# A graph network's second layer: edge features loaded into the ring, and gathers that add node rows to them

## The chip, the cores and the metric

The kernel runs on one core of a Trainium2 chip. The metric is the device time of one execution in microseconds; the kernel before takes 4083.93 us (median of 10 runs, 4080.28 to 4091.4). A core has TensorE (PE in the profile, with its weight loads PEld), VectorE (DVE), ScalarE (ACT), GpSimd (POOL) and SyncE (SP), each with its own instruction queue, and 16 DMA engines that all queues share. Here SP issues the plain loads and stores, and GpSimd issues the indirect gathers.

## What is computed

There are 12500 nodes with 128 features each and 200000 edges, sorted by destination. Two graph layers run one after the other, each followed by a residual addition and a normalization. The first is an attention layer. The second, cut to what matters:

```python
def _L1_gnn_ref(node_feat, edge_feat, src, dst, W1, b1, W2, b2):
    m = node_feat[src] + edge_feat
    neigh = jax.ops.segment_sum(m, dst, num_segments=node_feat.shape[0])
    h = 2.0 * node_feat + neigh
    h = h @ W1 + b1
    h = jnp.where(h > 0, h, 0.01 * h)
    return h @ W2 + b2
...
x = _layernorm(x + _L0_gnn_ref(x, edge_index, ...), axis=-1)
x = _layernorm(x + _L1_gnn_ref(x, edge_attr_128, src, dst, ...), axis=-1)
```

For every edge the second layer adds the source node's row and the edge's own feature row, both of 128 float32 numbers, and sums the result over the edges of each destination node.

## The kernel before, in words

The edges are cut into 112 chunks of 1792 edges (`CE` = 128 partitions x `T` = 14 tiles; the last chunk has 9 tiles). A tile is 128 edges, one per partition. Because edges are sorted by destination, a chunk touches a run of fewer than 128 destination nodes, so that the sum of a tile over its edges is one TensorE product: a 128x128 matrix of zeros and ones (edge by node, `od`), times the 128x128 rows of the tile, accumulated in PSUM (`ps`) over the tiles of the chunk. A node whose edges run over the end of a chunk is carried to the next chunk in a small product (`pc`).

A gather of one tile is one indirect DMA on GpSimd's queue (line 66, in `gather`): it reads 128 rows of 512 bytes from a table in HBM at the addresses in `srcs`, and writes them to one tile of a chunk's place in SBUF. A chunk is 14 such instructions, 64 KB each. The places are a ring of six (`ring`, `RING` = 6); chunk `c` uses place `c % 6`. Both layers gather through the same function and the same ring. The first layer gathers from `x_pad` and `xl_d`; its result `x1` is stored to `x1_d` in HBM by SP (line 567, in `norm2`), and stays in SBUF as `x1w`. The second layer gathers from `x1_d`, so that its first gather has to wait for the last of those stores.

The second layer is written out by hand in program order (the last loop of `fast_path`). Step `c` issues the load of the edge features of chunk `c + 2` (`load1`, lines 801 to 816, on SP, 896 KB), the 14 gathers of chunk `c + 1` (GpSimd), the making of `od` for chunk `c + 1` (`edges1`, on ScalarE, lines 240 and 241), and then the products of chunk `c` (`sums1`, line 823 on). Edge features go into a tile `ea` of their own, of which there are three. In `sums1` each tile takes two products with the same `od`, one with the edge features (line 827) and one with the gathered rows (line 828):

```python
nc.tensor.matmul(ps, od[:, t, :], ea[:, t, :], start=(t == 0), stop=False)
nc.tensor.matmul(ps, od[:, t, :], got[:, t, :], start=False, stop=(t == tiles[c] - 1))
```

Then VectorE adds twice the node's own row (line 833) and the carried row, and every fourth chunk `finish1` runs the two weight products, the normalization, and the stores of the output on SP (line 869). Those stores take their start row from a register that SP loads. The last chunk's output goes out by one indirect store on GpSimd (line 873).

Waits follow from the data. Each engine takes its queue in order, and an instruction whose operands are not ready holds up all behind it on its engine. A gather waits for the readers of its place in the ring (the products of the chunk six earlier) and, since eight completion counters are used in turn for GpSimd's DMAs, for the gather eight before it.

Of the kernel before, what the change touches and what calls it, by code (L numbers as in the profile page):

```python
# [8 lines left out]
F32 = mybir.dt.float32  # L9
# [3 lines left out]
OP = mybir.AluOpType  # L13
# [3 lines left out]
P = 128  # L17
D = 128
# [6 lines left out]
T = 14  # L25
# [4 lines left out]
RING = 6  # L30
# [6 lines left out]
def gnn_kernel(ctx: ExitStack, tc: tile.TileContext, a: dict, out: bass.AP):  # L37
# [3 lines left out]
    nc = tc.nc  # L41
    N = out.shape[0]
    E = a["edge_attr_128"].shape[0]
    NCH = a["dst_rows"].shape[0]
# [4 lines left out]
    tiles = [T] * (NCH - 1) + [-(-(E - (NCH - 1) * CE) // P)]  # L49
# [6 lines left out]
    srcs = const.tile([P, NCH, T], I32, name="srcs")  # L56
# [2 lines left out]
    nc.scalar.dma_start(srcs[:, 1:EARLY], src_of[:, 1:EARLY])  # L59
    ring = [const.tile([P, T, D], F32, name=f"got{i}") for i in range(EARLY)]  # L60

    def gather(table, c):

        got = ring[c % RING]
        for t in range(tiles[c]):
            nc.gpsimd.indirect_dma_start(  # L66
                out=got[:, t, :], out_offset=None, in_=table[:N, :],
                in_offset=bass.IndirectOffsetOnAxis(ap=srcs[:, c, t:t + 1], axis=0))
        return got

    for c in range(EARLY):
        gather(a["x_pad"], c)
# [30 lines left out]
    x1_d = dram.tile([NB * P + P, D], F32, name="x1_d")  # L103
# [109 lines left out]
    with tc.If(fits > 0) as cond:  # L213
        fast_path(tc, a, out, locals())
# [5 lines left out]
def fast_path(ctx: ExitStack, tc: tile.TileContext, a: dict, out: bass.AP, g: dict):  # L220
    nc = tc.nc
    N, E, NCH, groups, group_of = (g[k] for k in ("N", "E", "NCH", "groups", "group_of"))
    n0i, srcs, rel, same, lastf, thru, nid, khot, ident, wlr, xl_d, x1_d = (g[k] for k in (
        "n0i", "srcs", "rel", "same", "lastf", "thru", "nid", "khot", "ident", "wlr", "xl_d", "x1_d"))
    nnid, nrel, iota, rows, w12, b1, att, heads, tiles, ring, gather = (g[k] for k in (
        "nnid", "nrel", "iota", "rows", "w12", "b1", "att", "heads", "tiles", "ring", "gather"))
# [6 lines left out]
    def first_node(c, most=N):  # L233
        return nc.values_load(n0i[0:1, c:c + 1], engines=[ET.SP], min_val=0, max_val=most)

    def edge_by_node(od, c, t0, m):


        for t in range(t0, t0 + m):
            nc.scalar.activation(od[:, t, :], iota[:, 0, :], AF.Abs, bias=nrel[:, c, t:t + 1])  # L240
        nc.scalar.activation(od[:, t0:t0 + m, :], od[:, t0:t0 + m, :], AF.Relu, bias=1.0, scale=-1.0)  # L241

    def layernorm(w, of, n):
        st = w.tile([P, G, 6], F32, name="st")
        mv = w.tile([P, G, 2], F32, name="mv")
        for j in range(n):
            nc.vector.bn_stats(st[:, j, :], of[:, j, :])
            nc.vector.bn_aggr(mv[:, j, :], st[:, j, :])
        sd = w.tile([P, G], F32, name="sd")
        nc.scalar.activation(sd[:, :n], mv[:, :n, 1], AF.Sqrt, bias=eps)  # L250
        nc.vector.reciprocal(sd[:, :n], sd[:, :n])
        for j in range(n):
            nc.vector.tensor_scalar(of[:, j, :], of[:, j, :], mv[:, j, 0:1], sd[:, j:j + 1],
                                    op0=OP.subtract, op1=OP.mult)


    with tc.tile_pool(name="ew", bufs=2) as ew, \
# [425 lines left out]
        c, k, pool = NCH - 2, len(pairs) - 1, nc.gpsimd  # L683
# [112 lines left out]

    with tc.tile_pool(name="gw", bufs=2) as gw, \
            tc.tile_pool(name="gp", bufs=1, space=bass.MemoryType.PSUM) as gp:
        eas, gots, hs, ods = {}, {}, {}, {}

        def load1(c):
            ea = gw.tile([P, T, D], F32, name="ea", bufs=3)
            left = E - c * CE
            if left >= CE:
                nc.sync.dma_start(ea, a["edge_attr_128"][c * CE:(c + 1) * CE, :].rearrange(
                    "(p t) d -> p t d", t=T))
            else:
                m = tiles[c]
                full, more = left // m, left % m
                nc.vector.memset(ea[full // 32 * 32:, :m], 0.0)  # L810
                nc.sync.dma_start(ea[:full, :m], a["edge_attr_128"][c * CE:c * CE + full * m, :].rearrange(
                    "(p t) d -> p t d", t=m))
                if more:
                    nc.sync.dma_start(ea[full:full + 1, :more, :], a["edge_attr_128"][
                        None, c * CE + full * m:E, :])
            eas[c] = ea

        def edges1(c):
            ods[c] = gw.tile([P, T, P], F32, name="od")
            for t in range(0, tiles[c], 7):  # L820
                edge_by_node(ods[c], c, t, min(7, tiles[c] - t))

        def sums1(c):
            ea, got, od = eas.pop(c), gots.pop(c), ods.pop(c)
            ps = gp.tile([P, D], F32, name="ps", bufs=2)
            for t in range(tiles[c]):
                nc.tensor.matmul(ps, od[:, t, :], ea[:, t, :], start=(t == 0), stop=False)  # L827
                nc.tensor.matmul(ps, od[:, t, :], got[:, t, :], start=False, stop=(t == tiles[c] - 1))  # L828
            grp, j = group_of[c]
            if j == 0:  # L830
                hs[grp] = gw.tile([P, G, D], F32, name="h")
            h = hs[grp]
            nc.vector.scalar_tensor_tensor(h[:, j, :], x1w[:, c, :], 2.0, ps, op0=OP.mult, op1=OP.add)  # L833
            if c > 0:
                nc.vector.tensor_add(h[0:1, j, :], h[0:1, j, :], eas[-1])
            if c + 1 < NCH:
                ns = gw.tile([P, D], F32, name="ns")
                nc.scalar.copy(ns, ps)  # L838
                pc = gp.tile([1, D], F32, name="pc", bufs=2)
                nc.tensor.matmul(pc, khot[:, c:c + 1], ns, start=True, stop=True)  # L840
                eas[-1] = pc
            if j == grp[1] - 1:
                finish1(grp)

        def finish1(grp):
            c0, n = grp
            h, x1 = hs.pop(grp), x1w[:, c0:c0 + n, :]
            pT = gp.tile([P, G, P], F32, name="pT")
            for j in range(n):
                nc.tensor.transpose(pT[:, j, :], h[:, j, :], ident)  # L850
            hT = gw.tile([P, G, P], F32, name="hT")
            nc.scalar.copy(hT[:, :n], pT[:, :n])
            pu = gp.tile([P, G, P], F32, name="pu")
            nc.tensor.matmul(pu[:, :n], w12[:, 0, :], hT[:, :n], start=True, stop=True)
            z = gw.tile([P, G, P], F32, name="z")
            nc.scalar.activation(z[:, :n], pu[:, :n], AF.Identity, bias=b1)
            nc.vector.scalar_tensor_tensor(z[:, :n], z[:, :n], 0.01, z[:, :n],
                                           op0=OP.mult, op1=OP.max)
            po = gp.tile([P, G, D], F32, name="po")
            for j in range(n):  # L860
                nc.tensor.matmul(po[:, j, :], z[:, j, :], w12[:, 1, :], start=True, stop=True)
            nc.vector.tensor_add(x1, x1, rows["L1_gnn_b2"].to_broadcast([P, n, D]))
            y = gw.tile([P, G, D], F32, name="y")
            nc.vector.tensor_add(y[:, :n], po[:, :n], x1)
            layernorm(gw, y, n)
            for j in range(n):
                c = c0 + j
                if c + 1 < NCH:
                    nc.sync.dma_start(out[ds(first_node(c, N - P), P), :], y[:, j, :])
                else:  # L870
                    rows_i = gw.tile([P, 1], I32, name="rows_i", bufs=1)
                    nc.vector.tensor_copy(rows_i, nid[:, c:c + 1])
                    nc.gpsimd.indirect_dma_start(  # L873
                        out=out[:, :], out_offset=bass.IndirectOffsetOnAxis(ap=rows_i[:, 0:1], axis=0),
                        in_=y[:, j, :], in_offset=None, bounds_check=N - 1, oob_is_err=False)

        load1(0)
        load1(1)
        gots[0] = gather(x1_d, 0)
        edges1(0)  # L880
        for c in range(NCH):
            if c + 2 < NCH:
                load1(c + 2)
            if c + 1 < NCH:
                gots[c + 1] = gather(x1_d, c + 1)
                edges1(c + 1)
            sums1(c)

# [471 lines left out]
```

## Time and profile before

| what | us |
|---|---|
| median of 10 runs | 4083.93 |
| the profiled execution, its own time | 4089.8 |
| its span, first to last instruction | 4088.0 |
| the first gather of the second layer starts | 2113.70 |
| the last one starts | 4070.05 |
| TensorE busy | 3189.4 |
| GpSimd busy | 3002.5 |
| VectorE busy | 1821.7 |
| ScalarE busy | 1822.0 |

The mean granted TensorE clock is 0.804 of full speed. Busy time is summed over both layers, which have different limits, so that a row of the table of groups has to be read beside the timeline of its layer. A group's row gives line, engine, operation, output and inputs, shape and count, then busy time and mean ns of one, and then the engine's idle time just before them with what ended it. In the timeline of an engine, the bracket behind an instruction is the gap in front of it and what is taken to have released it. The profile's instruction interval of a gather is the time in which GpSimd issues it; the data land later.

### The profile page before, as it was taken

What the parts mean: (1) busy time and instruction counts of PE and PEld (TensorE: products, weight loads), DVE (VectorE), ACT (ScalarE), POOL (GpSimd) and SP (SyncE); (2) the same over time, 40 slices, a digit from 0 to 9 for tenths busy, and PEclk for the clock granted to TensorE, in tenths of its full rate; (3) what the DMA queues carried; (4) which work ended last, traced back from release to release, by engine and by line L of the source; (5) the groups of instructions that cost most, each with busy time, mean ns of one, the idle gap of its engine ahead of it and who ended that gap; (6) DMA issues with size and microseconds to landing.
All of it is one profiled execution on the core that took longest, in us unless ns stands there. A gap on an engine that the chain in (4) does not pass through costs nothing. (4 is left out here: it accounts for less than half of the span.)

```text
span 4088.0 us, 58612 instructions
## 1 busy us (share of the span) xinstructions
PE 3189.4 (78%) x18282; PEld 2616.7 (64%) x18394; DVE 1821.7 (45%) x6069; ACT 1822.0 (45%) x4397; POOL 3002.5 (73%) x3150
## 2 busy tenths in 40 slices
PE   7888888888888888888866677677777776676766
PEld 6777777777777777777755556555555555555555
DVE  4778777777777777777750101010010101010101
ACT  3555555555555555555543333334343333333342
POOL 7677777777777777777537777777777777777776
PEclk8888888888888888888877776777777777777677
DMA  7333333333333333333213333333333333333332
GB/s 237 97 114 104 114 104 112 114 115 111 106 115 104 114 114 114 106 112 114 89 65 110 108 112 94 119 101 121 100 120 102 112 110 112 110 95 117 101 121 74
DMA packets 235165, 451.14 MB, mean 110 GB/s; under 512 B 66040, under 2 KB 124281, under 8 KB 234843
## 3 DMA queue, kind: packets, MB, share of 16 engines
q0 software_dynamic: 100064, 205.10, 18.0%
q1 hardware_dynamic: 133627, 238.52, 17.1%
q10 hardware_dynamic: 1152, 3.67, 0.3%
q8 instruction: 148, 2.42, 0.2%
q14 instruction: 174, 1.43, 0.1%
HBM read 425.96 MB, written 21.10 MB: 109 GB/s over the span
## 5 line engine op out<-in xcount | busy, mean ns | idle before, releaser
L66 POOL DMA_INDIRECT got<-x_d,srcs x1563 | 1481.3, 948 | 482.9 <-DMA got<-x_d,srcs 196.0
L66 POOL DMA_INDIRECT got<-xl_d,srcs x1507 | 1447.4, 960 | 487.0 <-issue 189.1
L828 PE MATMUL ps<-got,od 128*128 128x128 f32 x3126 | 852.7, 364 | 434.9 <-DMA got<-x_d,srcs 429.7
L828 PEld LDWEIGHTS ps<-got,od 128*128 128x128 f32 x3126 | 627.9, 249 | 576.2 <-DMA got<-x_d,srcs 572.9
L827 PE MATMUL ps<-ea,od 128*128 128x128 f32 x3126 | 777.5, 340 | 17.1 <-ACT od L241 17.1
L833 DVE SCALAR_TENSOR_TENSOR h<-x1w,ps 128x128 f32<-128x128 f32 x112 | 32.3, 288 | 1549.2 <-PE ps L828 1549.2
L827 PEld LDWEIGHTS ps<-ea,od 128*128 128x128 f32 x3126 | 636.5, 252 | 42.5 <-issue 42.5
L470 PE MATMUL ps<-val,od 128*128 128x137 f32 x3080 | 596.7, 376 | 0.0
L470 PEld LDWEIGHTS ps<-val,od 128*128 128x128 f32 x3080 | 579.6, 280 | 0.5 <-issue 0.3
L240 ACT ACTIVATE od<-iota,nrel 128x128 f32<-128x128 f32 x1563 | 478.5, 388 | 0.8 <-DVE x1w L522 0.8
L838 ACT COPY ns<-ps 128x128 f32<-128x128 f32 x111 | 29.5, 266 | 946.3 <-DVE h L833 946.3
L378 PEld LDWEIGHTS sc<-attm,lk 128*128 128x128 f32 x3126 | 387.3, 193 | 91.5 <-DVE lk L360 82.3
L378 PE MATMUL sc<-attm,lk 128*128 128x4 f32 x3126 | 413.2, 253 | 14.7 <-DVE lk L360 2.4
L359 ACT ACTIVATE lk<-ph 128x512 f32<-128x512 f32 (+1 forms) x447 | 242.2, 542 | 392.6 <-PE ph L352 392.6
L360 DVE TENSOR_TENSOR lk<-ph,lk 128x512 f32<-128x512 f32 (+1 forms) x447 | 278.0, 622 | 193.3 <-ACT lk L359 192.2
L352 PE MATMUL ph<-odt,parts 128*128 128x512 bf16 (+1 forms) x1229 | 305.0, 352 | 7.3 <-ACT odt L342 1.1
L368 DVE TENSOR_TENSOR od<-bank,rel 128x512 f32<-128x512 f32 (+1 forms) x440 | 268.2, 610 | 57.3 <-PE ps L470 57.3
L459 DVE TENSOR_TENSOR val<-got,bank 128x512 f32<-128x512 f32 (+1 forms) x447 | 273.6, 613 | 1.2 <-ACT lks L306 0.5
L349 PE MATMUL ph<-ident,got 128*128 128x128 f32 x1563 | 259.5, 283 | 0.0
L340 ACT ACTIVATE odt<-row,nnid 128x1024 bf16<-128x1024 int32 x224 | 233.1, 1041 | 0.0
L349 PEld LDWEIGHTS ph<-ident,got 128*128 128x128 f32 x1563 | 193.0, 154 | 47.5 <-issue 26.0
L241 ACT ACTIVATE od<-od 128x896 f32<-128x896 f32 x224 | 212.2, 947 | 7.1
(163 smaller groups left out, 3329.1 us busy)
## 6 DMA issues: line engine op xcount, KB each, us to landing
ea<-in_edge_attr SPq DMA_DIRECT2D x111, 896.0 KB
row<-in_dst_rows SPq DMA_DIRECT2D x329, 256.0 KB
got<-x_d,srcs POOLq DMA_INDIRECT x1563
got<-xl_d,srcs POOLq DMA_INDIRECT x1507
row<-in_dst_rows SPq DMA_DIRECT2D x109, 128.0 KB
xg<-in_x_pad SPq DMA_DIRECT2D x112, 64.0 KB
x_d<-x1w SPq DMA_DIRECT2D x112, 64.0 KB
out<-y SPq DMA_DIRECT2D x111, 64.0 KB
```

Source lines behind the costliest of these rows:

```text
L66: nc.gpsimd.indirect_dma_start(out=got[:, t, :], out_offset=None, in_=table[:N, :], in_offset=bass.IndirectOffsetOnAxis(ap=srcs[:, c, t:t ...
L240: nc.scalar.activation(od[:, t, :], iota[:, 0, :], AF.Abs, bias=nrel[:, c, t:t + 1])
L349: nc.tensor.matmul(ph[:, t * P:(t + 1) * P], got[:, t0 + t, :], ident, start=(t == 0), stop=False, is_transpose=True)
L352: nc.tensor.matmul(ph[:, :m * P], parts[:, k, :], odt[:, t0 * P:(t0 + m) * P], start=False, stop=(k == 2))
L359: nc.scalar.mul(lk[:, :m * P], ph[:, :m * P], 0.2)
L360: nc.vector.tensor_max(lk[:, :m * P], ph[:, :m * P], lk[:, :m * P])
L368: nc.vector.tensor_tensor(live["od", c][:, t0:t0 + m, :], bank[:, None, :P].to_broadcast([P, m, P]), rel[:, c, t0:t0 + m, None].to_broadca ...
L378: nc.tensor.matmul(live["sc", c][:, :, t0 + t], lk[:, t * P:(t + 1) * P], attm, start=True, stop=True)
L459: nc.vector.tensor_mul(vh[:, :, :, :C], live["got", c][:, t0:t0 + m, :].rearrange("p t (h c) -> p t h c", h=H), wts[:, t0:t0 + m, :, None] ...
L470: nc.tensor.matmul(ps, od[:, t, :], v[:, t, :], start=(t == 0), stop=(t == tiles[c] - 1))
L827: nc.tensor.matmul(ps, od[:, t, :], ea[:, t, :], start=(t == 0), stop=False)
L828: nc.tensor.matmul(ps, od[:, t, :], got[:, t, :], start=False, stop=(t == tiles[c] - 1))
```

## The change

In the second layer, `load1` puts the edge features of a chunk straight into the chunk's place in the ring instead of into a tile `ea`. The gathers of the chunk are given the operation "add", so that each row read from `x1_d` is added to the 512 bytes that stand at its destination, where the plain gather overwrote them. What stands in the place when the chunk's gathers are done is the sum of node row and edge row, and `sums1` makes one product per tile with it. The first layer's gathers keep the plain form (`OP.bypass`).

Loads are issued three chunks ahead instead of two: 0, 1 and 2 ahead of the loop, and `c + 3` in step `c`. A chunk's first gather now also waits for the chunk's load, and a load waits for the products of the chunk that last used the place, which is six chunks earlier. The three `ea` tiles are gone, and the dictionary `eas`, which also held the carried row, is called `over`.

```diff
-    def gather(table, c):
+    def gather(table, c, op=OP.bypass):
 
         got = ring[c % RING]
         for t in range(tiles[c]):
             nc.gpsimd.indirect_dma_start(
                 out=got[:, t, :], out_offset=None, in_=table[:N, :],
-                in_offset=bass.IndirectOffsetOnAxis(ap=srcs[:, c, t:t + 1], axis=0))
+                in_offset=bass.IndirectOffsetOnAxis(ap=srcs[:, c, t:t + 1], axis=0), compute_op=op)
         return got
...
         def load1(c):
-            ea = gw.tile([P, T, D], F32, name="ea", bufs=3)
+            ea = ring[c % RING]
...
         def sums1(c):
-            ea, got, od = eas.pop(c), gots.pop(c), ods.pop(c)
+            got, od = gots.pop(c), ods.pop(c)
             ps = gp.tile([P, D], F32, name="ps", bufs=2)
             for t in range(tiles[c]):
-                nc.tensor.matmul(ps, od[:, t, :], ea[:, t, :], start=(t == 0), stop=False)
-                nc.tensor.matmul(ps, od[:, t, :], got[:, t, :], start=False, stop=(t == tiles[c] - 1))
+                nc.tensor.matmul(ps, od[:, t, :], got[:, t, :], start=(t == 0), stop=(t == tiles[c] - 1))
...
-        load1(0)
-        load1(1)
-        gots[0] = gather(x1_d, 0)
+        for c in range(3):
+            load1(c)
+        gots[0] = gather(x1_d, 0, OP.add)
         edges1(0)
         for c in range(NCH):
-            if c + 2 < NCH:
-                load1(c + 2)
+            if c + 3 < NCH:
+                load1(c + 3)
             if c + 1 < NCH:
-                gots[c + 1] = gather(x1_d, c + 1)
+                gots[c + 1] = gather(x1_d, c + 1, OP.add)
                 edges1(c + 1)
             sums1(c)
```

More of the change, by code (lines that the diff above doesn't have):

```diff
@@ L798, in fast_path @@
             tc.tile_pool(name="gp", bufs=1, space=bass.MemoryType.PSUM) as gp:
-        eas, gots, hs, ods = {}, {}, {}, {}
+        over, gots, hs, ods = {}, {}, {}, {}
         def load1(c):
-            ea = gw.tile([P, T, D], F32, name="ea", bufs=3)
+            ea = ring[c % RING]
             left = E - c * CE
@@ L815, in load1 @@
                         None, c * CE + full * m:E, :])
-            eas[c] = ea
         def edges1(c):
@@ L834, in sums1 @@
             if c > 0:
-                nc.vector.tensor_add(h[0:1, j, :], h[0:1, j, :], eas[-1])
+                nc.vector.tensor_add(h[0:1, j, :], h[0:1, j, :], over[-1])
             if c + 1 < NCH:
@@ L840, in sums1 @@
                 nc.tensor.matmul(pc, khot[:, c:c + 1], ns, start=True, stop=True)
-                eas[-1] = pc
+                over[-1] = pc
             if j == grp[1] - 1:
```

## The prediction

> **What bounds the kernel now.** I read the page's table of instruction groups first, then the timeline of GpSimd in the second layer, then busy time by stretch, then the two ends of the layer. The second layer begins when the last x1_d store has landed, and the change touches nothing ahead of it. In the table of groups (busy us, mean ns of one, then idle time before and what ended it):
>
> ```profile
> L66 POOL DMA_INDIRECT got<-x_d,srcs x1563 | 1481.3, 948 | 482.9 <-DMA got<-x_d,srcs 196.0
> ...
> L828 PE MATMUL ps<-got,od 128*128 128x128 f32 x3126 | 852.7, 364 | 434.9 <-DMA got<-x_d,srcs 429.7
> ...
> L827 PE MATMUL ps<-ea,od 128*128 128x128 f32 x3126 | 777.5, 340 | 17.1 <-ACT od L241 17.1
> ```
>
> The product with the gathered rows (line 828) waits 435 us for gathers to land; the product with the edge features (line 827) hardly waits. GpSimd shows 483 us of idle time, but the timeline says what that is (start, duration, in brackets the gap ahead and its releaser):
>
> ```profile
> 3004.80 0.94 POOL L66 DMA_INDIRECT got<-x_d,srcs  x1 [0.30 <-DMA got<-x_d,srcs]
> 3006.04 0.95 POOL L66 DMA_INDIRECT got<-x_d,srcs  x1 [0.30 <-issue]
> 3007.30 0.94 POOL L66 DMA_INDIRECT got<-x_d,srcs  x1 [0.30 <-issue]
> 3008.55 0.94 POOL L66 DMA_INDIRECT got<-x_d,srcs  x1 [0.30 <-issue]
> ```
>
> Every gather takes 0.94 us and follows the last after 0.30 us, whatever releaser is named: no wait, but the pitch of back-to-back gathers. The layer's first one starts at 2113.70 and its last at 4070.05, so the mean pitch is 1956.35 / 1562 = 1.2525 us, and 1563 gathers fill 1957 us of the layer. Busy time by stretch (PE, PEld, DVE, ACT, POOL, then clock, DMA share and GB/s) agrees:
>
> ```profile
> 2113.70:4070.00 1956.30, 1379.11 (x6856) 1122.92 (x6857) 202.55 (x675) 740.61 (x1981) 1480.32 (x1562) 0.73 0.35 109
> ...
> 3017.00:3019.00 2.00, 2.00 (x12) 2.00 (x11) 0.00 (x0) 0.00 (x0) 1.42 (x2) 0.50 0.17 47
> ```
>
> TensorE is busy 1379 of 1956 us and catches up in every chunk (in the stretch from 3003 to 3010 it consumes each tile as it lands and then waits 0.5 to 1.4 us for the next). The DMA engines work 35% of the layer, and 17% where only gathers run. So the layer is set by how fast GpSimd issues gathers.
>
> At the two ends:
>
> ```profile
> 2111.80 1.31 SPq L805 DMA_DIRECT2D ea<-in_edge_attr  x3
> ...
> 2113.70 1.06 POOL L66 DMA_INDIRECT got<-x_d,srcs  x1 [6.85 <-DMA x_d<-x1w]
> ...
> 2117.32 0.77 PE L827 MATMUL ps<-ea,od 128*128 128x128 f32 x2 [17.10 <-ACT od L241]
> ```
>
> ```profile
> 4070.05 0.94 POOL L66 DMA_INDIRECT got<-x_d,srcs  x1 [0.30 <-PE ps L827]
> ...
> 4073.14 0.49 PE L828 MATMUL ps<-got,od 128*128 128x128 f32 x2 [1.16 <-DMA got<-x_d,srcs]
> ...
> 4079.99 1.03 POOL L873 DMA_INDIRECT out<-y,rows_i  x1 [8.99 <-POOLq L213]
> ```
>
> The first gather waits for the x1_d store alone, while loads are on their way; the last one lands 3.1 us after its start and one product follows it.
>
> **The change, part by part.**
>
> *Products removed.* 3126 line-827 instructions, 777.5 us of TensorE. They lie beside the gathers: per chunk they take 28 x 0.25 = 7 us of a 17.5 us chunk in which TensorE ends up waiting anyway. Even the last tile's product with edge features runs ahead of the last landing (it is 828 that waits at 4073.14). Worth 0 us, at most the 0.4 us of a pair at the end. A higher granted clock, which is 0.73 in the layer, gives nothing either while TensorE waits.
>
> *Loads into the ring.* The same 112 chunk loads, now into one of six ring places instead of three ea buffers, requested three chunks ahead. A load into the place of chunk c-3 waits for that chunk's products, done some three chunks before, and on SP it stands behind at most one group's output stores (a group's finish takes about 8 us in the tail's rows). The new wait of each chunk's first gather on its load has two to three chunks, 35 to 50 us, in hand. Cost 0, as long as a 0.92 MB load takes the 2 to 4 us it takes now; without that lead each chunk would lose those microseconds, 112 x 4 = 448 us.
>
> *The first gather.* Here there is no lead: it was held by the x1_d store until 2113.70, and now also needs load 0, issued at 2111.80. From 2112 the DMA engines moved 137, 222, 287 and 423 GB/s in successive microseconds; 0.92 MB are through at 2115.6 if load 0 comes first, and at 2120 if the three loads issued together share (2.75 MB). So 2 to 6 us; I take 3, nearer the first, since they are issued one after the other on one queue. Behind this gather stand all 1562 others, so it counts in full.
>
> *The gathers add.* 1563 gathers, all on the path, each on GpSimd's queue ahead of the next. A plain gather deals with two sets of 128 row places (those read in x1_d, those written in the ring). An adding one has to read the ring rows as well: three sets. No row of this trace has an adding transfer, so I bound it. From below: the extra read is produced beside the rest or is a mere flag, 0 us (a gain is excluded: nothing the gather did is dropped). From above: it costs as much as a second gather with its gap, 1.2525 us. Nearer is the busy part of the one gather, 0.944 us, if reading the ring rows costs like the whole of today's work. I take three sets in place of two, the work growing by half with the 0.30 us gap kept: 0.944 / 2 = 0.472 us, pitch 1.72 us. That is 1563 x 0.472 = 738 us; with 0.944 it is 1475, with 1.2525 it is 1958.
>
> Two pages bear on exactly this term and disagree. The Trainium skill, "DMA: Bandwidth & Descriptors", Anatomy of one DMA, calls descriptor generation small and says many descriptors go out before the extra cost shows; by that the term is about 0 and the time 4087. The 1.25 us pitch above, set by generation and not by moving data, speaks against taking it as small. The Trainium skill, "GPSIMD Engine Reference", When to use GPSIMD, says that one core emits the read descriptors and another the write descriptors; if so a second read per row would double the reading core's list, and the sum would be up to 5562. No row here shows either core alone.
>
> *Moving the data.* Queue 0 used 18.0% of 16 x 4088 us for 100064 packets, 0.118 us each; 3126 gathers make 32 packets each, two per engine with four rows in each, 0.235 us of an engine per gather. Three accesses in place of two, or even three times the packets (0.71 us), stay below 1.25 us next to the loads (0.92 MB at 423 GB/s is 2.2 us a chunk, 0.155 us per gather). Cost 0 unless rows go one by one, which is a rival below.
>
> *Sum.* -0 + 0 + 3 + 738 = +741 us. The profiled execution took 4089.8 us (span 4088.0), 5.9 us above the median of 4083.93, so it would be 4831 there and 4825 as a median.
>
> **The rivals.**
>
> *The add is free to issue* (ends on the other side). The pitch stays 1.2525 us, and only the start is paid: 4083.9 + 3 = 4087, within the 0.2% (8 us) that a measurement of this kernel can tell from no change. For it: 0.94 us may be mostly fixed, and no row varies the number of rows. Against it: a program for three lists in place of two must write more. It decides if the extra work per gather is under 0.003 us on GpSimd, since every 0.005 us is 8 us.
>
> *The DMA engines become the bound.* If a row that is added travels by itself and pays a packet for each of its two reads and its write, an engine needs 8 x 3 x 0.118 = 2.82 us per gather, with the loads 2.98: 1563 x 1.73 = 2700 us more, 6784. It takes over once an engine's time passes 1.10 us, 4.7 times today's. Against it: today's rows travel in fours.
>
> *The products were the bound after all.* Halving them would then free up to 435 us, the wait of 828. Against it: that wait is for gathers, and gathers keep 1.25 us. This would give 3650; I see no place for it.
>
> **How the numbers follow.** The add costs between nothing and a second gather: 0.67, forecast 4825, its own range 4320 (0.15 us each) to 6045 (1.2525 us). Free to issue: 0.18. Beyond 6045, by the engines or by a much longer routine: 0.13. Products the bound or some other gain: 0.02. The range from 4080 to 6050 leaves out 0.15; both ends are the bounds of the one unknown price, and the upper is not brought down because nothing in the trace is nearer to an adding transfer than a gather. Faster 0.02; within 0.2% 0.15; slower 0.83 (a free add with a longer start counts here).
>
> **What would show it.** In the changed kernel's timeline the start-to-start distance of adding gathers is the whole answer: 1.72 us by the forecast, 1.25 if the add is free. The busy part should grow with the gap still 0.30 us; a gap that grows, released by gathers eight earlier, with a DMA share near 0.9 would show the engines as the bound. The first gather should start near 2117 on the old time scale. TensorE should wait for gathers on nearly every tile, its busy share in the layer falling from 70% to below 35%. The forecast fails if the adding gather's pitch is outside 1.35 to 2.5 us, or if the wait of a chunk's first gather on its load shows up in every chunk instead of only the first.

## The result, and the profile after

| | before | after |
|---|---|---|
| median, us | 4085.62 (28 runs, 4080.28 to 4091.4) | 5035.03 (8 runs, 5033.57 to 5041.68) |
| span of the profiled execution, us | 4088.0 | 5033.9 |
| mean granted TensorE clock | 0.804 | 0.668 |
| a gather of the second layer, median ns | 944 | 1553 |
| TensorE busy, us | 3189.4 | 3131.6 |
| GpSimd busy, us | 3002.5 | 3951.2 |

The changed kernel is slower: 1.2327 times the time before, 95% interval 1.2316 to 1.2338. TensorE lost 3126 instructions (two for each of 1563 products) and gained no time for the kernel. GpSimd gained 949 us of busy time, and the span grew by 946.

The table of groups of the changed kernel (busy us, mean ns of one, then idle time before and what ended it):

```profile
L66 POOL DMA_INDIRECT got<-x_d,srcs x1563 | 2429.8, 1555 | 486.9 <-issue 392.1
L826 PE MATMUL ps<-got,od 128*128 128x128 f32 x3126 | 1130.2, 480 | 1457.0 <-DMA got<-x_d,srcs 1456.0
```

The gathers' row grew from 1481.3 to 2429.8 us with the idle time ahead of them unchanged (482.9 and 486.9 us). The one product left waits 1456 us for gathers, where it waited 430 before. The timeline of GpSimd in the second layer, at about the same time in the layer as the four rows of the prediction (start, duration, in brackets the gap ahead and its releaser):

```profile
3004.56 1.55 POOL L66 DMA_INDIRECT got<-x_d,srcs  x1 [0.31 <-issue]
3006.41 1.55 POOL L66 DMA_INDIRECT got<-x_d,srcs  x1 [0.30 <-issue]
3008.27 1.55 POOL L66 DMA_INDIRECT got<-x_d,srcs  x1 [0.30 <-issue]
3010.13 1.55 POOL L66 DMA_INDIRECT got<-x_d,srcs  x1 [0.30 <-issue]
```

The gap is still 0.30 us and each gather is 0.6 us longer. The profile shows no wait of GpSimd; the instruction itself takes longer. Whether something holds GpSimd up inside the instruction, these rows can't say; e5, e7 and e8 look for that. The layer's stretch from its first to its last gather (length, then busy time of PE, PEld, DVE, ACT, POOL, then clock, DMA share and GB/s) and its two ends:

```profile
2112.26:5016.72 2904.46, 1326.87 (x3737) 842.78 (x3737) 199.42 (x675) 736.64 (x1970) 2428.21 (x1563) 0.52 0.40 73
```

```profile
2106.73 3.26 SPq L805 DMA_DIRECT2D got<-in_edge_attr  x6
...
2112.26 1.65 POOL L66 DMA_INDIRECT got<-x_d,srcs  x1 [10.68 <-DMA got<-in_edge_attr]
...
2121.03 0.77 PE L826 MATMUL ps<-got,od 128*128 128x128 f32 x2 [26.08 <-DMA got<-x_d,srcs]
```

```profile
5016.72 1.55 POOL L66 DMA_INDIRECT got<-x_d,srcs  x1 [0.30 <-issue]
...
5020.07 0.80 PE L826 MATMUL ps<-got,od 128*128 128x128 f32 x2 [1.15 <-DMA got<-x_d,srcs]
...
5027.57 1.04 POOL L871 DMA_INDIRECT out<-y,rows_i  x1 [9.30 <-POOLq L213]
```

The mean pitch is 2904.46 / 1562 = 1.8594 us against 1.2525. The first gather now starts 5.53 us after the loads are issued (2112.26 - 2106.73), where it was 1.90 (2113.70 - 2111.80), and its releaser is a load of edge features instead of the x1_d store. The end is the same: the last gather lands 3.35 us after its start (3.1 before).

The two spans balance: the loads ahead of the layer were issued 5.07 us earlier, the start took 3.63 us more, 1562 pitches took 948.1 us more (2904.46 - 1956.35), and what follows the last gather's start took 0.8 us less (17.2 instead of 18.0). That is -5.1 + 3.6 + 948.1 - 0.8 = 945.9 us, the difference of the spans. The 5 us at the start are variation from run to run: in e1, e4, e10 and e11 below, whose first layer is the same and whose gathers don't add, the second layer's first gather starts anywhere from 2105.9 to 2117.2.

### The profile page after: what moved, and what is told of

The parts are those of the page before. It is cut to its first block, busy times and chain, and to the rows that moved or that the text cites. A ratio compares the mean times of both kernels' runs of the same rounds, so it can differ in the third digit from the quotient of the medians.

```text
span 5033.9 us, 52910 instructions
## 1 busy us (share of the span) xinstructions
PE 3131.6 (62%) x15156; PEld 2332.0 (46%) x15268; DVE 1818.2 (36%) x6069; ACT 1821.7 (36%) x4397; POOL 3951.2 (78%) x3150
## 3 DMA queue, kind: packets, MB, share of 16 engines
q0 software_dynamic: 275120, 205.10, 24.1%
## 5 line engine op out<-in xcount | busy, mean ns | idle before, releaser
L66 POOL DMA_INDIRECT got<-x_d,srcs x1563 | 2429.8, 1555 | 486.9 <-issue 392.1
L826 PE MATMUL ps<-got,od 128*128 128x128 f32 x3126 | 1130.2, 480 | 1457.0 <-DMA got<-x_d,srcs 1456.0
L826 PEld LDWEIGHTS ps<-got,od 128*128 128x128 f32 x3126 | 753.4, 309 | 1842.2 <-DMA got<-x_d,srcs 1801.5
L342 ACT ACTIVATE odt<-odt 128x1024 bf16<-128x1024 bf16 x224 | 212.3, 948 | 3.6
L352 PEld LDWEIGHTS <-parts 128*128 128x128 bf16 x1341 | 131.7, 98 | 48.0 <-ACT parts L320 1.5
```

What stands on the lines that cost most here:

```text
L66: nc.gpsimd.indirect_dma_start(out=got[:, t, :], out_offset=None, in_=table[:N, :], in_offset=bass.IndirectOffsetOnAxis(ap=srcs[:, c, t:t ...
L352: nc.tensor.matmul(ph[:, :m * P], parts[:, k, :], odt[:, t0 * P:(t0 + m) * P], start=False, stop=(k == 2))
L826: nc.tensor.matmul(ps, od[:, t, :], got[:, t, :], start=(t == 0), stop=(t == tiles[c] - 1))
```

## Experiments

The theory: the whole loss is the time in which GpSimd issues an adding gather, and the removed products are worth nothing. The rivals: the DMA engines hold the gathers back; the new wait on the loads does; or the products were worth something that the adding gathers then ate up. If the theory holds, there is a second question, which the forecast rested on: is the price paid for each row in the lists, or for each instruction?

Lines of the form "x1563: 940/945/1280, 2110.5 to 4068.7" are about the second layer's gathers: their count, the shortest, median and longest duration in ns, and the starts of the first and the last one in us (the last entry is not used). The times of e2, e3, e4, e5, e8, e8b, e9, e10 and e11 are of one execution each.

### e1: the changed kernel without the add

```diff
-        gots[0] = gather(x1_d, 0, OP.add)
+        gots[0] = gather(x1_d, 0)
...
-                gots[c + 1] = gather(x1_d, c + 1, OP.add)
+                gots[c + 1] = gather(x1_d, c + 1)
```

> The changed kernel with its second-layer gathers back in the plain form: they overwrite the edge features that were loaded into the ring, so the edge features are left out of the sums. Everything else of the change stays: loads into the ring, three chunks ahead, one product per tile, the first gather waiting for load 0. Theory (issuing an adding gather costs GpSimd 0.607 us more, 1562 x 0.607 = 948 us, and nothing else of the change matters): pitch 1.25 us, 4085 to 4089 us. Rival 'ring' (the loads into the ring and the waits they bring cost the time): about 5035 us. Rival 'engines' (an adding gather makes 144 packets in place of 32 and the DMA engines hold GpSimd back): 4085 to 4089 too.

Measured: 4090.55 us (4087.34 to 4097.44) beside 4086.26, a ratio of 1.0017 (1.0007 to 1.0026), where 4085 to 4089 were expected. Its gathers, its row of the product in the table of groups, and its layer's stretch:

```profile
L66 POOL DMA_INDIRECT got<-x_d,srcs x1563: 940/945/1280, 2110.5 to 4068.7; - x196
```

```profile
L826 PE MATMUL ps<-got,od 128*128 128x128 f32 x3126 | 1044.9, 463 | 596.0 <-DMA got<-x_d,srcs 569.9
```

```profile
2110.50:4068.70 1958.20, 1240.31 (x3736) 813.82 (x3736) 202.58 (x675) 736.83 (x1970) 1482.32 (x1563) 0.53 0.32 108
```

Loads into the ring, the new wait and half the products are all here, and the gather is back at 945 ns and the pitch at 1958.2 / 1562 = 1.2536 us. So everything but the add costs 4 us, about the longer start (5.49 us from the loads' issue to the first gather here), and the removed products buy nothing. They don't even relieve TensorE much: 3120 fewer instructions took only 139 us off its busy time (1379.11 to 1240.31), while the granted clock fell from 0.73 to 0.53 and an instruction of a product took 463 ns instead of 364 (line 828) and 340 (line 827).

### e2: the kernel before with only the add

```diff
-    def gather(table, c):
+    def gather(table, c, op=OP.bypass):
...
-                in_offset=bass.IndirectOffsetOnAxis(ap=srcs[:, c, t:t + 1], axis=0))
+                in_offset=bass.IndirectOffsetOnAxis(ap=srcs[:, c, t:t + 1], axis=0), compute_op=op)
...
-                gots[c + 1] = gather(x1_d, c + 1)
+                gots[c + 1] = gather(x1_d, c + 1, OP.add)
```

> The kernel before with one thing changed: its second-layer gathers add to whatever stands in the ring, so each place keeps the sum of all that was gathered into it and the result is left wrong in that way. Loads go to ea two chunks ahead, two products per tile. Theory: pitch 1.86 us and 4086 + 948 = 5034 us, so the removed products are worth nothing. Rival 'ring': about 4086 us. If the halving of the products did help the changed kernel: over 5040 us.

Measured: 5032.93 us, beside 5035.03 for the full change. Its gathers:

```profile
L66 POOL DMA_INDIRECT got<-x_d,srcs x1563: 1545/1554/1671, 2108.3 to 5013.7; - x196
```

All of the loss is in the add: with two products per tile, own tiles for the edge features, and no wait of a gather on a load (the first gather waits for the x1_d store, 1.94 us after the loads' issue), the time is that of the full change within 0.04%. That removes the wait on loads and the products as causes.

### e3, e4, e9, e10: fewer rows in each gather

Each layer-2 gather has 64 or 32 of its 128 rows, adding or plain. The number of instructions is kept, so that rows and instructions can be told apart. For 64 rows, adding (e3; in e4 `OP.bypass`; in e9 and e10 32 rows):

```diff
-                out=got[:, t, :], out_offset=None, in_=table[:N, :],
-                in_offset=bass.IndirectOffsetOnAxis(ap=srcs[:, c, t:t + 1], axis=0), compute_op=op)
+                out=got[:n, t, :], out_offset=None, in_=table[:N, :],
+                in_offset=bass.IndirectOffsetOnAxis(ap=srcs[:n, c, t:t + 1], axis=0), compute_op=op)
...
-                gots[c + 1] = gather(x1_d, c + 1, OP.add)
+                gots[c + 1] = gather(x1_d, c + 1, OP.add, 64)
```

> The changed kernel with adding gathers of 64 rows instead of 128 (partitions 64 to 127 keep the edge features alone, so half the node rows are left out of the sums). Beside the plain 64-row run it splits the price of an add into a part per row and a part per instruction. If all is per row: busy part 1.553 / 2 = 0.78 us, pitch 1.08, about 5035 - 1563 x 0.777 = 3820 us. If all is per instruction: 1.553 us and 5035. My guess for the add's extra 0.609 us is that it is per row, so that this run's busy part is 0.30 us above the plain 64-row run's. Rival 'engines': half the packets, so the hold-up goes and the pitch equals the plain 64-row one.

> The same with plain gathers of 64 rows (the edge features of partitions 0 to 63 are overwritten and left out, and the node rows of partitions 64 to 127). If a plain gather's 0.944 us is all per row: 0.47 us, pitch 0.77, about 4086 - 1563 x 0.472 = 3348 us, or later if TensorE or the loads become the bound; if it is all per instruction: 0.944 us and 4088. My guess: 0.62 us busy, pitch 0.92, about 3580 us.

> Adding gathers of 32 rows (three quarters of the node rows are left out). The 128-row and 64-row runs give 1.553 and 1.420 us, a line of 1.287 us per instruction plus 2.08 ns per row; the plain ones give 0.862 us plus 0.64 ns per row. If that line holds down to 32 rows: busy part 1.354 us, pitch 1.66, about 5035 - 1563 x 0.199 = 4724 us. If the 64-row point was held up by something that does not depend on rows and the true price per row is larger: well under 1.35 us.

> Plain gathers of 32 rows (the edge features of partitions 0 to 31 and the node rows of the others are left out). The plain line through 128 and 64 rows is 0.862 us per instruction plus 0.64 ns per row: busy part 0.883 us, pitch 1.185, about 4088 - 1563 x 0.0615 = 3992 us; more if loads or products set a floor by then.

The gathers of e3, e4, e9 and e10 in turn:

```profile
L66 POOL DMA_INDIRECT got<-x_d,srcs x1563: 1411/1420/1884, 2109.7 to 4815.5; - x196
```

```profile
L66 POOL DMA_INDIRECT got<-x_d,srcs x1563: 897/903/1419, 2112.6 to 4010.4; - x196
```

```profile
L66 POOL DMA_INDIRECT got<-x_d,srcs x1563: 1331/1338/1507, 3470.9 to 6037.7; - x196
```

```profile
L66 POOL DMA_INDIRECT got<-x_d,srcs x1563: 862/867/1120, 2117.2 to 3948.5; - x196
```

| rows | plain, ns | adding, ns | difference |
|---|---|---|---|
| 128 | 945 (e1) | 1553 (after) | 608 |
| 64 | 903 (e4) | 1420 (e3) | 517 |
| 32 | 867 (e10) | 1338 (e9) | 471 |

The times were 4836.41 (e3), 4031.12 (e4) and 3968.87 us (e10). e9 took 6058.88 us.

e5, e7, e8 and e9 ran together on another chip, on which the kernel before itself takes 5927.59 us; of these runs only the second layer's gathers are compared here.

Both pure theories of e3 fail: half the rows were to give 3820 us if the price is paid by the row, 5035 if by the instruction. e4 misses its 3580 by 451 us in the same direction. The guess for the add's extra, that it is paid by the row, misses too: 0.30 us were expected at 64 rows, and 0.517 were measured. Most of the price is paid by the instruction. Through the points for 128 and 64 rows, a plain gather takes about 0.86 us and 0.65 ns more for each row (42 / 64), an adding one 1.29 us and 2.08 ns for each row (133 / 64). The extra of an adding gather is then, as an estimate from these lines, some 0.42 us for the instruction and 0.18 us for its 128 rows. The points for 32 rows test the lines. They predict 883 and 1354 ns; 867 and 1338 were measured, both 16 ns lower, so the lines are near but not exact (e10 took 3968.87 us where 3992 were expected). Below 32 rows nothing was measured.

The rows' number also shows in the queues. GpSimd's queue of the changed kernel, of e3 and of e4 (packets, MB, share of 16 engines):

```profile
q0 software_dynamic: 275120, 205.10, 24.1%
```

```profile
q0 software_dynamic: 175088, 153.88, 16.6%
```

```profile
q0 software_dynamic: 100064, 153.88, 13.8%
```

A plain gather makes 32 packets whatever its rows: the kernel before and e4 both have 100064. With the first layer's packets taken off as half of those, about 50030, an adding gather of 128 rows makes (275120 - 50030) / 1563 = 144 packets and one of 64 rows (175088 - 50030) / 1563 = 80: one for each row and 16 more. With 32 rows (e9, 125072 packets in all) it is 48, only 16 more than a plain gather makes, and the gather still takes 471 ns longer. So the extra is not in proportion to the packets.

### e5: the same rows, half the bytes

```diff
+            rows = table[:N // 2, :].rearrange("n (h d) -> (n h) d", h=2) if half else table[:N, :]
             nc.gpsimd.indirect_dma_start(
-                out=got[:, t, :], out_offset=None, in_=table[:N, :],
+                out=got[:, t, :D // 2 if half else D], out_offset=None, in_=rows,
```

> The changed kernel with adding gathers of 128 rows of 256 bytes instead of 512 (wrong rows, and half of each row is left out). Theory: issuing does not depend on bytes, busy part 1.553 us, about 5035 us. Rival 'engines': half the bytes per packet, so the busy part falls, towards 0.94 us if moving the data is what holds GpSimd back.

Measured: 6398.79 us on the chip named above. Its gathers in the timeline:

```profile
4999.62 1.55 POOL L67 DMA_INDIRECT got<-x_d,srcs  x1 [0.31 <-issue]
5001.47 1.55 POOL L67 DMA_INDIRECT got<-x_d,srcs  x1 [0.30 <-issue]
```

256 bytes per row instead of 512 leave the 1.55 us as they are; the median of all 1563 is 1554 ns, as in e2. The data moved by a gather doesn't set its price on GpSimd.

### e7 and e7b: half the dose

Odd chunks are done the new way, even ones the old way with two products, so that half the gathers add (779 of 1563: 55 odd chunks of 14 tiles and the last one with 9).

```diff
-            ea = ring[c % RING]
+            ea = ring[c % RING] if c % 2 else gw.tile([P, T, D], F32, name="ea", bufs=3)
+            if c % 2 == 0:
+                eas[c] = ea
...
+                if c % 2 == 0:
+                    nc.tensor.matmul(ps, od[:, t, :], ea[:, t, :], start=(t == 0), stop=False)
+                nc.tensor.matmul(ps, od[:, t, :], got[:, t, :], start=(t == 0 and c % 2 == 1),
+                                 stop=(t == tiles[c] - 1))
...
-                gots[c + 1] = gather(x1_d, c + 1, OP.add)
+                gots[c + 1] = gather(x1_d, c + 1, OP.bypass if c % 2 else OP.add)
```

> Odd chunks as in the changed kernel (features into the ring, adding gathers, one product per tile), even chunks as in the kernel before (features into ea, plain gathers, two products). 779 of the 1563 gathers add. Theory: every adding gather costs its 0.607 us on GpSimd whatever stands around it: 4086 + 779 x 0.607 = 4559 us, pitch 1.86 in odd chunks and 1.25 in even ones. Rival 'engines': adds that come in bursts of 14 with plain gathers between would be absorbed in part, clearly under 4559, with adding gathers shorter than 1.55 us.

> The half dose again (odd chunks as in the changed kernel, even chunks as in the kernel before, 779 adding gathers), since the first time it ran on a chip on which the kernel before takes 5928 us. On a chip on which it takes 4086: 4086 + 779 x 0.607 = 4559 us by the theory, clearly less by the rival 'engines'.

e7b measured 4565.09 us (4560.8 to 4568.69) beside 4087.24, a ratio of 1.1175 (1.1156 to 1.1193), where 4559 were expected. The dose is linear: half of 949 is 475, and 478 were measured. The timeline where an odd chunk's gathers end and an even one's begin, and where the next odd chunk begins:

```profile
3021.90 1.55 POOL L66 DMA_INDIRECT got<-x_d,srcs  x1 [0.30 <-issue]
3023.75 1.55 POOL L66 DMA_INDIRECT got<-x_d,srcs  x1 [0.30 <-issue]
3025.60 1.00 POOL L66 DMA_INDIRECT got<-x_d,srcs  x1 [0.31 <-issue]
3026.91 0.97 POOL L66 DMA_INDIRECT got<-x_d,srcs  x1 [0.30 <-issue]
3028.18 0.94 POOL L66 DMA_INDIRECT got<-x_d,srcs  x1 [0.30 <-DMA got<-x_d,srcs]
...
3041.93 0.94 POOL L66 DMA_INDIRECT got<-x_d,srcs  x1 [0.30 <-PE ps L829]
3043.18 1.57 POOL L66 DMA_INDIRECT got<-x_d,srcs  x1 [0.30 <-PE ps L829]
```

The first adding gather after 14 plain ones takes the full time at once (1.57 us at 3043.18), and two instructions after the last one the plain time is back. That also speaks against the engines as the cause: a backlog in them should lengthen the gathers little by little.

e7, the same kernel on the other chip, took 5939.62 us beside 5927.59 there, a ratio of 1.0018 (0.9989 to 1.0048), which no theory expected. Its gathers:

```profile
L66 POOL DMA_INDIRECT got<-x_d,srcs x1563: 943/1333/1605, 3446.5 to 5882.8; - x196
```

The mean pitch is (5882.8 - 3446.5) / 1562 = 1.5597 us, as in e7b ((4543.0 - 2108.6) / 1562 = 1.5585). So its second layer is as long as in e7b; only the layer ahead of it is longer, with the first gather of the second layer at 3446.5 instead of 2108.6. The kernel before takes as long there in all. If its first layer was as long there as in e7, its second was too, and can't have been set by gathers of 1.25 us. That is an inference, as no profile of the kernel before was had there. e5 and e8, in which all 1563 gathers add, took 471 and 480 us more than the kernel before on that chip. So the loss of 949 us holds for chips of the usual speed.

### e8 and e8b: twice the loads

The changed kernel, which loads each chunk's features a second time, into a tile that nobody reads:

```diff
             if left >= CE:
+                spare = gw.tile([P, T, D], F32, name="spare", bufs=3)
+                nc.sync.dma_start(spare, a["edge_attr_128"][c * CE:(c + 1) * CE, :].rearrange(
+                    "(p t) d -> p t d", t=T))
```

> The changed kernel, and every full chunk's edge features loaded a second time to tiles that nobody reads: 0.92 MB more per chunk on the same DMA engines, about 2.2 us of them per chunk of 26 us. Theory (GpSimd's issue sets the pitch): the pitch stays 1.86 us, about 5035 us plus 2 to 4 us for the first gather, whose load stands behind one more. Rival 'engines': each gather pays for its share of the added load, 0.155 us, so 5035 + 242 = about 5277 us, and adding gathers longer than 1.55 us.

> The changed kernel with every full chunk's edge features loaded twice, again, for its whole time on a chip on which the kernel before takes 4086 us. Theory: pitch 1.86 us, 5037 to 5040 us (the first gather's load stands behind one more). Rival 'engines': about 5277 us.

e8b measured 5037.83 us, where 5037 to 5040 were expected if the engines have room and 5277 if they are the bound. The layer's stretch from 2200 to 4900 in e8b, and then in the changed kernel:

```profile
2200.00:4900.00 2700.00, 1209.64 (x3476) 775.42 (x3476) 183.61 (x622) 686.59 (x1833) 2257.06 (x1453) 0.52 0.48 109
```

```profile
2200.00:4900.00 2700.00, 1233.62 (x3475) 782.85 (x3474) 183.98 (x623) 685.03 (x1829) 2257.28 (x1453) 0.52 0.40 73
```

The engines moved 109 instead of 73 GB/s in the same time, with the same 1453 gathers. They aren't the bound, and more of their load doesn't lengthen a gather. e8 says the same on the other chip, where it took 6407.12 us:

```profile
L66 POOL DMA_INDIRECT got<-x_d,srcs x1563: 1545/1554/1680, 3481.8 to 6388.0; - x196
```

### e11: the kernel before once more

The kernel before, unchanged. It was meant to give a profile of the kernel before on the slower chip, and to test whether its second layer is longer there.

> The kernel before once more, unchanged, for a profile of it beside the runs of a second chip, on which the kernel before takes about 5928 us. Theory: the pitch of plain gathers in the second layer is 1.25 us where GpSimd sets it. If this run is on such a chip and 5928 us is right, its second layer takes about 2480 us, and then something other than GpSimd sets it there: the waits of the gathers and of TensorE will say what. On a chip like the first: 4086 us and 1.25 us throughout.

It ran on yet another chip, of the usual speed, and took 4080.72 us, beside 4082.16:

```profile
L66 POOL DMA_INDIRECT got<-x_d,srcs x1563: 940/944/1297, 2105.9 to 4061.3; - x196
```

The pitch is (4061.3 - 2105.9) / 1562 = 1.2519 us. It repeats the profile before, and what happens on the slower chip stays open.

## Why the prediction was right, and where a term was off

*The bound.* Right. GpSimd's issue of gathers set the layer before and sets it after. Pitch times count explains the layer in every run with a profile. That the kernel gets slower because its gathers, one behind the other on GpSimd's queue, get longer is what e2 isolates.

*Products removed, 0 us.* Right: e1 has them removed and is 4 us slower than before, e2 has them kept and is as slow as the full change. The remark that TensorE's busy share would fall below 35% was wrong: it is 1326.87 / 2904.46 = 46%. It was taken that half the products need half the time. Instead the granted clock fell from 0.73 to 0.52, and an instruction of a product took 480 ns instead of 364 and 340; mean times clock is about the same (266 and 248 ns before, 250 after).

*Loads into the ring, 0 us.* Right. The gaps ahead of the gathers stay 0.30 us (none behind the layer's first gather is over 0.31), and the wait on a load shows only at the layer's start. e8b shows that there was room for twice the loads.

*The first gather, 3 us.* Right: 3.6 us.

*The gathers add, 0.472 us each.* This is the term that was mis-sized. Measured: 0.607 us each (1.8594 - 1.2525), 948 us in all and not 738. The 210 us between them are the forecast's miss: 4825 forecast, 5035 measured. The value lay inside the bounds set for it, 0 to 1.2525 us. The step that failed is "three sets in place of two, the work growing by half": it takes the 0.944 us as work that grows with the lists of rows. Runs e3, e4, e9 and e10 show otherwise: with a quarter of the rows a plain gather still takes 867 of 945 ns and an adding one 1338 of 1553. By the lines through 128 and 64 rows some nine tenths of a plain gather (0.86 of 0.944 us) and eight tenths of an adding one (1.29 of 1.553) are paid whatever the number of rows, and the add brings a fixed 0.42 us of its own. What GpSimd does in those fixed times, no run shows. That the forecast came within 4.2% of the time is therefore partly luck: the argument that gave 0.472 us is not how the price is made up. And the range, 4080 to 6050, was as wide as the bounds of the one unknown price, so that its holding says little about the size.

The estimates that were worked out there from two pages of the Trainium skill both miss it. "DMA: Bandwidth & Descriptors", Anatomy of one DMA, by which the term would be about 0, is off by the whole 948 us. "GPSIMD Engine Reference", When to use GPSIMD, from which a doubling of one core's list was worked out, gave 5562, 527 us too much; the extra that grows with the rows, which such a list could explain, is only 0.18 of 0.6 us. What that page itself states, that one core emits the read and another the write descriptors, no run here shows.

*Moving the data, and the engines as a rival.* Half of the rival's premise came true, and its price did not. Rows that are added do go one by one, but in 144 packets a gather instead of 32, not in the 384 (24 for each of 16 engines) that a packet for each read and write would make. And the queue's share rose only to 24.1%: 0.241 x 16 x 5033.9 = 19410 us of engine time, less some 5900 for the first layer (half of 0.18 x 16 x 4088), is 13500 us, or 13500 / 1563 / 16 = 0.54 us of an engine per gather. With 9 packets for each engine that is 0.06 us a packet, where the rival took 24 packets at 0.118. It was to take over past 1.10 us.

*The free add, a chance of 0.18,* is excluded by e2, and *the products as the bound,* by e1.

No version that gathers all rows came out faster than the kernel before by more than the spread of its runs. The ones that are faster (e4, e10) gather fewer rows.

## What to carry to other kernels

Before work is moved into a gather, look at which engine issues the gathers: here an indirect DMA of 128 rows costs GpSimd about 0.9 us as an instruction and 0.42 more for being an adding one. Its 128 rows add less (by the lines above 0.08 us plain, 0.27 adding), and its bytes nothing that e5 could see. A row in which each instruction follows the last after the same short gap, under changing releasers, is a queue at its own pace, and every nanosecond added to that instruction is paid by the count; taking work off an engine that waits for that queue buys nothing. Where the price of an instruction's form is in no row of the trace, one run with only that form switched on (e2) gives it.

## What was not expected of the hardware

With half of TensorE's products gone from a layer that waits for something else, the granted clock was 0.53 instead of 0.73 (e1) and each product took longer, so that busy time fell by 139 us only. e2 shows the same without fewer products: there TensorE waits longer for the same work, the layer's clock is 0.56, and its busy time grows from 1379 to 1840 us. The number of busy microseconds is no measure of how much work TensorE has left here.

Adding gathers are split into one packet for each row (144 packets for 128 rows), plain ones are not (32), and each of these packets takes about half the engine time that was taken for them (0.06 us instead of 0.118).

One chip ran the kernel before in 5927.59 us. In the profiles of other kernels there, the first layer was the long part: in e8's stretch from 500 to 3000 us, the waits (engine, what waits, releaser: us in all, times, longest) were led by

```profile
POOL got L66 <- PE pn L304: 682.9, 53, 14.7
ACT lk L359 <- remote: 434.2, 54, 13.7
```

The gathers' issue times in the second layer were the same there to a nanosecond or two (1554 ns in e5 and e8). ScalarE standing still 54 times for 8 us each (434.2 / 54), for reasons that the trace files under "remote", are the sign of it: e5, e7 and e9 have such waits in that layer too, and the changed kernel and e8b, on chips of the usual speed, have none. Why that chip does so stays open.
